# Queue order of the scan's loads, and GpSimd's part of a group norm a tick later

## Chip, cores and metric

The kernel runs on one core of a Trainium2 chip. The metric is the device time of one execution in microseconds (us), the median of several runs. Engines are named as the profile names them: PE (TensorE matmuls) and PEld (its weight loads), DVE (VectorE), ACT (ScalarE), POOL (GpSimd) and SP (SyncE, which issues nearly all DMAs).

## What is computed

Four layers on x of 4 images x 128 channels x 64 x 64 pixels, float32, each `x = x + layer(group_norm(x))`:

```
x = x + attention(gn(x))      # one head over 4096 pixels, 128 channels
x = x + conv5x5(gn(x))        # 25 taps, built from tables of weights
x = x + ssm(gn(x))            # 1x1 conv, two state-space scans, 1x1 conv
x = x + conv3x3(gn(x))
```

The third layer is what the change is about. Channels 0 to 63 run forward over the 4096 pixels, channels 64 to 127 backward; each channel has 64 states:

```
xc    = silu(causal_conv4(u))
delta = softplus(xc @ Wd + bd);  Bm = xc @ WB;  Cm = xc @ WC
h[t]  = exp(delta[t] * A) * h[t-1] + (delta[t] * xc[t]) * Bm[t]
y[t]  = sum over states (h[t] * Cm[t]) + D * xc[t]
```

## The kernel before

One program order is written out by hand (a manual schedule), and every engine runs its own queue in that order. There are two streams in it. `scan_core` (L1394) writes the scan, tick by tick. A generator, `images` in `program`, writes everything else ("the work"): attention, 5x5 convolution, the operands of the scan (`scan_prep`, `scan_operands`), and for images whose scan is over the last layer (`stage`, `end`, `back`).

**Ticks.** A tick is one step on a tile of 128 x 1024: 32 channels x 4 states on the partitions, 1024 pixels along. An image has 256 ticks: 4 chunks of pixels (c) x 2 directions (d) x 16 groups of states (q) x 2 groups of channels (g), g innermost. A "chunk-direction" (c, d) is thus 32 ticks. For tick i:

- `load` (L1428), on SP: for q = 0 the tiles `de` (delta) and `dx` (delta times xc) of this (c, d, g), each 512 KB, three buffers each; for g = 0 the rows `b` and `c` of B and C, 512 KB each, three buffers each, which serve two ticks; for q = 0 and g = 0 also `xc`, two DMAs of 128 KB into one tile.
- `drive` (L1469), on POOL: `db = dx * b` (L1472), three buffers.
- `decay` (L1454), on ACT: `da = exp(de * a)` (L1465) into PSUM.
- `recur` (L1474), on DVE: the scan `h = da * h + db` (L1482), and for two ticks of three the product with the C row (L1485).
- `weigh` (L1500), on POOL: that product for the other ticks (L1503); while PE has "wide" banks it is every i with i % 3 = 2.
- `collect` (L1505), on PE: sums over states (L1521), four ticks at a time; `keep` (L1490), on ACT, saves the last state of a chunk.

The loop at the end of `scan_core` (L1567) sets the order in step i, in short:

```
do(drive, i + 2); do(keep, i - 1); do(decay, i + 1, 0); do(recur, i)
do(weigh, i - 1); do(take, i - 4); do(preset, i - 4); do(collect, i - 3)
yield i
do(decay, i + 1, 1); do(load, i + AHEAD)      # AHEAD = 4
yield i
```

Within `load(i)` the order is de, dx (if q = 0), b, c (if g = 0), xc (if q = g = 0). Since each tile has a fixed number of buffers, a DMA into one waits until the last reader of what was in it is done; SP waits, and all DMAs written later wait behind it.

**The work between the ticks.** At each of the two yields of a step the driver adds half of `pace` to a credit and takes work until the credit is used; each piece of work yields its own cost in us. `PACES` gives the pace during the ticks of images 0 to 3. During the ticks of image b (b < 3), attention, convolution and operands of image b + 1 are written; during those of image 3, the last layers of images 0 to 2. When (b, "operands", c) is in `ready`, the operands of chunk c have been written; `before(b)` (L1782) is called four ticks before an image's first tick and takes work without ticks until the first chunk's operands are there.

**The group norm.** `group_norm` (L353) ends a long chain of small DVE instructions with a transpose `back` (L385), then two small products on POOL, `rs` (L387, a power of -0.5) and `nb` (L388), and yields. It is called for attention ("a"), the 5x5 convolution ("e"), the scan ("s") and the last layer ("m"). Nine of these calls fall among the ticks: e and s of images 1 to 3, m of images 0 to 2.

Of the kernel before, what the change touches and what calls it, by code (L numbers as in the profile page):

```python
# [32 lines left out]
P = 128  # L33
GROUPS = 32
GN_EPS = 1e-5
CH = 1024
MM = 512
HALF = P // 2
# [4 lines left out]

PRODUCT, VALUES, HOP, SLOT, AHEAD = 0.86, 0.9, 1.7, 0.7, 4
PACES = 2.65, 2.61, 2.6, 1.5


BQ, BK, BX, BP, CONVB, BD, DSKIP, MAINB, CONVW, ALOG = 0, 1, 2, 3, 4, 5, 6, 7, 8, 12  # L50
# [3 lines left out]
def conv_preact_kernel(  # L54
# [16 lines left out]
    nc = tc.nc  # L71
# [3 lines left out]
    NST = vecs.shape[1] - ALOG  # L75
    KC = 4
    SG, NI = 32, P // 32
# [14 lines left out]
    pools, ready = {}, set()  # L92
# [49 lines left out]
    NK, NQ = P // SG, NST // NI  # L142
# [167 lines left out]
    NRING = 8  # L310


    gn_work = const.tile([P, 2, 2 * 32], F32, name="gn_work")
    gn_sums = const.tile([P, 2, 32 // gsz], F32, name="gn_sums")

# [37 lines left out]
    def group_norm(st, name):  # L353


        def tile(tag, *shape):
            return small.tile([P, *shape], F32, tag=f"gn_{tag}", name=f"{tag}_{name}")

        by_sums = isinstance(st, Sums)
        if by_sums:  # L360
            st.aggregate()
        else:
            nc.vector.bn_aggr(gcols[:, :, 0], st.rearrange("p a b -> p (a b)"))
        turned, after = gn_work[:, 0], gn_work[:, 1]
# [12 lines left out]
        nc.vector.tensor_tensor(means, means, mean, ALU.add)  # L377
        nc.vector.tensor_tensor(means, means, means, ALU.mult)
        nc.vector.tensor_tensor(means, means, vars_, ALU.subtract if by_sums else ALU.add)
        total = gn_sums[:, 1]  # L380
        nc.vector.tensor_reduce(total, means, AX.X, ALU.add)
        wide = total.unsqueeze(2).to_broadcast([P, 32 // gsz, gsz])
        nc.vector.tensor_scalar(var, wide, 1.0 / gsz, GN_EPS, ALU.mult, ALU.add)
        back = tile("back", 2, 32)
        nc.vector.transpose(back.rearrange("p a b -> p (a b)"), after)  # L385
        rs, nb = tile("rs", 1), tile("nb", 1)
        nc.gpsimd.tensor_tensor(rs, back[:, 0, 0:1], mhalf, ALU.pow)  # L387
        nc.gpsimd.tensor_tensor(nb, back[:, 1, 0:1], rs, ALU.mult)  # L388
        yield HOP
        return rs, nb  # L390
# [30 lines left out]
    def attention_start(b, xn):  # L421

        if b == 0:
            st = stats_tile(f"a{b}")
            for i in range(NM):
                nc.vector.bn_stats(st[:, i, :], xn[:, bass.ts(i, MM)])
                yield 0.0
            gn = yield from group_norm(st, f"a{b}")
# [962 lines left out]
    KG = NK // 2  # L1391
    TICKS = NCH * 2 * NQ * KG

    def scan_core(mats4, ynds, before, widen, result):  # L1394


        ticks = [
            (b, c, d, q, g) for b in range(B)
            for c in range(NCH) for d in range(2) for q in range(NQ) for g in range(KG)
        ]  # L1400
        rows, rep, dbs, hcs, hold, yacc, xcs, last = {}, {}, {}, {}, {}, {}, {}, {}
# [21 lines left out]
        def at(i):  # L1423
            b, c, d, q, g = ticks[i]
            n = (d * KG + g) * NQ + q
            return slice(n, n + 1)

        def load(i):  # L1428
            b, c, d, q, g = ticks[i]
            (bmat, cmat), dd, dxd, xcd, _ = mats4[b]  # L1430
            if q == 0:
                assert (b, "operands", c) in ready
                for name, src in (("de", dd), ("dx", dxd)):
                    t = in_turn("rep", name, 3, [P, CH], f"{name}_{b}_{c}_{d}_{g}")
                    k = d * KG + g
                    src = src[c, k * SG : (k + 1) * SG].unsqueeze(1)
                    nc.sync.dma_start(t, src.to_broadcast([SG, NI, CH]))
                    rep[name, b, c, d, g] = t
            if g == 0:
                for name, src in (("b", bmat), ("c", cmat)):  # L1440
                    t = in_turn("rows", name, 3, [P, CH], f"{name}r_{b}_{c}_{d}_{q}")
                    n = d * NST + q * NI
                    nc.sync.dma_start(t, src[c, n : n + NI].unsqueeze(0).to_broadcast([SG, NI, CH]))
                    rows[name, b, c, d, q] = t
            if q == 0 and g == 0:
                t = in_turn("rows", "xc", 2, [P, MM], f"xcr_{b}_{c}_{d}")
                for h in range(CH // MM):
                    nc.sync.dma_start(
                        t[h * HALF : (h + 1) * HALF, :],
                        xcd[c, d * HALF : (d + 1) * HALF, bass.ts(h, MM)],  # L1450
                    )
                xcs[b, c, d] = t

        def decay(i, h):  # L1454
            b, c, d, q, g = ticks[i]
            if h == 0:
                das[i] = []
            elif "wide" in pools:
                return

            wide = "wide" in pools
            size = CH if wide else MM
            da = in_turn(*(("wide", "da", 2) if wide else ("s2", "half", 3)), [P, size], f"da_{i}_{h}")
            das[i].append(da)
            nc.scalar.activation(  # L1465
                da, rep["de", b, c, d, g][:, bass.ts(h, size)], AF.Exp, scale=a_neg[:, at(i)]
            )
# [93 lines left out]
        n = len(ticks)  # L1561

        def do(step, i, *args):
            if 0 <= i < n:
                step(i, *args)

        for i in range(-AHEAD, n + 4):  # L1567
            if (i + AHEAD) % TICKS == 0 and i + AHEAD < n:
                before((i + AHEAD) // TICKS)
            do(drive, i + 2)  # L1570
            do(keep, i - 1)
            late = i + 1 < n and i >= 0 and widen()
            if not late:
                do(decay, i + 1, 0)
            do(recur, i)
            if late:
                do(keep, i)
                late()
                do(decay, i + 1, 0)
            do(weigh, i - 1)  # L1580
            if i < n + 3:
                do(take, i - 4)
            do(preset, i - 4)
            do(collect, i - 3)
            yield i
            do(decay, i + 1, 1)
            do(load, i + AHEAD)
            yield i

    def scan_end(b, xs, st, yt, pieces):  # L1590
# [14 lines left out]
    def program(safe):  # L1605
        nonlocal more
        mats4, ynds, ends = {}, {}, {}
        ready.clear()
        ready.add("narrow")
        shared.clear()  # L1610
        if safe:
            nc.sync.dma_start(cs[:, :10, :], kept_sums)

        def load(tile, src):
            for c in range(NCH):
                nc.sync.dma_start(tile[:, bass.ts(c, CH)], src[:, bass.ts(c, CH)])
                yield 0.0
# [111 lines left out]
        with ExitStack() as es, tc.manual_schedule():  # L1729
# [49 lines left out]
            pools["hc"] = es.enter_context(tc.tile_pool(name=f"hc{safe}", bufs=8))  # L1779
            pace = PACES[0]  # L1780

            def before(b):  # L1782

                nonlocal pace
                while (b, "operands", 0) not in ready:
                    next(work)
                pace = PACES[min(b, len(PACES) - 1)]

            def result():

                while (B - 1, "staged") not in ready:
                    next(work, None)
                return ends[B - 1][2]

            credit = 0.0
            for i in scan_core(mats4, ynds, before, widen, result):
                if i % TICKS == 6 and i > TICKS:
                    ready.add((i // TICKS - 1, "scan"))
                if i == B * TICKS - TICKS // NCH + 6:
                    ready.update({(B - 1, "inner"), (B - 1, "lower")})  # L1800
                if i == B * TICKS - TICKS // NCH // 2 + 6:
                    ready.add((B - 1, "last"))
                credit = min(credit + pace / 2, pace)
# [22 lines left out]
    with tc.If(again > 0):  # L1826
        program(True)
# [59 lines left out]
```

## Time and profile before

| what | us |
|---|---|
| median of 3 runs (lowest, highest) | 4236.12 (4235.12, 4243.51) |
| the profiled execution | 4238.44 |
| its span in the profile | 4236.6 |
| first drive (L1472) starts | 675.0 |
| last drive starts | 4163.2 |
| POOL busy, of which drives and `weigh` | 3523.4, of which 2394.9 and 832.6 |
| DVE busy, of which scans of the four common forms and products | 3557.1, of which 2311.5 and 828.8 |
| PE busy | 3683.7 |

DMAs: 512 each of the b and c rows, 64 each of de and dx, all of 512 KB; one queue (q1 on the page) moves 736.99 MB of 740.97. The median time from issue to landing is 5.5 us for b, 4.2 for c, 5.2 for de, 6.4 for dx.

How to read the profile: it is one execution. A line of the waits reads "engine, output, line <- what ended the wait: us in total, times, longest". A line of the windows has the stretch, its length, then busy time and number of instructions of PE, PEld, DVE, ACT, POOL, the granted clock of PE, the share of the DMA engines and GB/s. A line of the timeline has the start, the time from start to end, engine, line, operation and tiles, how many equal instructions were merged, and in brackets the idle time before it and what ended it. Ends of matmuls are modelled, and spans on POOL are rough.

### The profile page before, as it was taken

What the parts mean: (1) busy time and instruction counts of PE and PEld (TensorE: products, weight loads), DVE (VectorE), ACT (ScalarE), POOL (GpSimd) and SP (SyncE); (2) the same over time, 40 slices, a digit from 0 to 9 for tenths busy, and PEclk for the clock granted to TensorE, in tenths of its full rate; (3) what the DMA queues carried; (4) which work ended last, traced back from release to release, by engine and by line L of the source; (5) the groups of instructions that cost most, each with busy time, mean ns of one, the idle gap of its engine ahead of it and who ended that gap; (6) DMA issues with size and microseconds to landing.
All of it is one profiled execution on the core that took longest, in us unless ns stands there. A gap on an engine that the chain in (4) does not pass through costs nothing. (4 is left out here: it accounts for less than half of the span.)

```text
span 4236.6 us, 49519 instructions
## 1 busy us (share of the span) xinstructions
PE 3683.7 (87%) x17628; PEld 2133.7 (50%) x17628; DVE 3557.1 (84%) x2554; ACT 2332.4 (55%) x3910; POOL 3523.4 (83%) x1683
## 2 busy tenths in 40 slices
PE   8999998999999879999999889999898466575666
PEld 4444444888883338887753267787633122121212
DVE  3832216999999979999999899999998899999996
ACT  3344316666664476666653766666645554544442
POOL 2533316999999979999999899999998899999995
PEclk9999999999999989999999999999999688787877
DMA  1120006555555576555555655555555755666562
GB/s 66 47 91 21 3 20 246 195 184 194 193 192 192 180 259 202 192 194 186 196 183 180 241 207 183 196 187 192 191 184 204 250 199 200 218 203 234 188 227 74
DMA packets 223725, 740.97 MB, mean 175 GB/s; under 512 B 29662, under 2 KB 30942, under 8 KB 223212
## 3 DMA queue, kind: packets, MB, share of 16 engines
q1 hardware_dynamic: 221548, 736.99, 50.1%
q8 instruction: 140, 2.29, 0.2%
q14 instruction: 117, 0.96, 0.1%
q10 hardware_dynamic: 1920, 0.73, 0.1%
HBM read 662.14 MB, written 75.47 MB: 174 GB/s over the span
## 5 line engine op out<-in xcount | busy, mean ns | idle before, releaser
L1472 POOL TENSOR_TENSOR db<-dx,br 128x1024 f32<-128x1024 f32 x1024 | 2394.9, 2367 | 170.3 <-DMA dx<-dxd 71.7
L1465 ACT ACTIVATE da<-de,a_neg 128x1024 f32<-128x1024 f32 (+1 forms) x1091 | 1161.5, 1065 | 396.5 <-DVE hc L1485 272.3
L1482 DVE TENSOR_TENSOR_SCAN da<-da,last,db 128x1024 f32<-128x1024 f32 (+1 forms) x501 | 1149.4, 2294 | 48.4 <-POOL db L1472 38.4
L1485 DVE TENSOR_TENSOR hc<-da,cr 128x1024 f32<-128x1024 f32 (+1 forms) x708 | 828.8, 1171 | 63.4 <-DVE da L1482 1.4
L1521 PE MATMUL y<-hc,sel 128*32 128x512 f32 x4096 | 609.0, 649 | 305.9 <-POOL hc L1503 226.1
L1503 POOL TENSOR_TENSOR hc<-hc,cr 128x1024 f32<-128x1024 f32 x352 | 832.6, 2365 | 4.4 <-ACT last L1498 3.0
L696 PE MATMUL sc<-r,x 128*128 128x256 f32 x3072 | 806.4, 388 | 27.6 <-ACT exchange L709 16.4
L717 PEld LDWEIGHTS acc<-v,exchange 128*128 128x128 f32 x6144 | 802.1, 192 | 46.4 <-issue 10.0
L717 PE MATMUL acc<-v,exchange 128*128 128x129 f32 x6144 | 804.8, 275 | 0.0
L696 PEld LDWEIGHTS sc<-r,x 128*128 128x128 f32 x3072 | 532.0, 192 | 191.9 <-ACT last L1498 41.1
L1482 DVE TENSOR_TENSOR_SCAN hc<-da,last,db 128x1024 f32<-128x1024 f32 (+1 forms) x267 | 596.0, 2232 | 6.1 <-POOL db L1472 5.5
L709 ACT ACTIVATE exchange<-sc 128x512 f32<-128x512 f32 x768 | 444.2, 589 | 225.5 <-PE sc L696 216.5
L1521 PEld LDWEIGHTS y<-hc,sel 128*32 128x32 f32 x4096 | 115.2, 113 | 658.2 <-POOL hc L1503 322.1
L1482 DVE TENSOR_TENSOR_SCAN da<-da,db 128x1024 f32<-128x1024 f32 (+1 forms) x171 | 376.6, 2203 | 22.7 <-ACT da L1465 12.9
L518 POOL TENSOR_TENSOR sidep<-sidep,exchange 128x512 f32<-128x512 f32 x120 | 172.6, 1439 | 245.2 <-ACT exchange L500 242.8
L1498 ACT COPY last<-da 128x1 f32<-128x1 f32 x512 | 80.5, 157 | 518.0 <-DVE hc L1485 517.2
L500 ACT ACTIVATE exchange<-sc 128x512 f32<-128x512 f32 x256 | 152.6, 596 | 253.7 <-PE sc L499 248.9
L518 DVE TENSOR_TENSOR sided<-sided,exchange 128x512 f32<-128x512 f32 x120 | 98.7, 823 | 211.6 <-ACT exchange L500 210.5
L506 PE MATMUL acc<-exchange,v 128*128 128x512 f32 x512 | 261.9, 594 | 0.9
L499 PE MATMUL sc<-r,x 128*128 128x512 f32 x512 | 262.0, 594 | 0.6 <-ACT r L482 0.6
L861 PE MATMUL pcm<-xpm,cs 128*128 128x512 f32 x432 | 211.0, 637 | 41.3 <-ACT xpm L393 41.3
L1482 DVE TENSOR_TENSOR_SCAN hc<-da,db 128x1024 f32<-128x1024 f32 (+1 forms) x85 | 189.5, 2230 | 5.7 <-ACT da L1465 5.7
(266 smaller groups left out, 3062.0 us busy)
## 6 DMA issues: line engine op xcount, KB each, us to landing
br<-bm SPq DMA_DIRECT2D x512, 512.0 KB, 5.5
cr<-cm SPq DMA_DIRECT2D x512, 512.0 KB, 4.2
de<-dd SPq DMA_DIRECT2D x64, 512.0 KB, 5.2
dx<-dxd SPq DMA_DIRECT2D x64, 512.0 KB, 6.4
xs<-in_x_dram SPq DMA_DIRECT2D x16, 512.0 KB, 7.4
xsd<-xs SPq DMA_DIRECT2D x16, 512.0 KB, 6.1
xcd<-xc SPq DMA_DIRECT2D x16, 512.0 KB, 4.6
bm<-bs SPq DMA_DIRECT2D x32, 256.0 KB, 5.3
```

The costliest lines, as they stand in the source:

```text
L499: nc.tensor.matmul(sc, xn[:, bass.ts(j, P)], rq[blk], start=True, stop=True)
L506: nc.tensor.matmul(acc[blk], v[:, j, :C], ring[:, u % NRING, :], start=j == 0, stop=j == NJT - 1)
L518: eng.tensor_tensor(s, s, ring[:, u % NRING, :], ALU.add)
L696: nc.tensor.matmul(sc[:, bass.ts(n, HM)], xn[:, bass.ts(2 * k + n, P)], rq[blk][:, cut], start=True, stop=True,)
L709: nc.scalar.activation(pt, sc, AF.Exp)
L717: nc.tensor.matmul(acc[part][:, bass.ts(t, CV)], ring[:, u % NRING, n * HM + t * P : n * HM + (t + 1) * P], v[:, 2 * k + n, :], start=(k, ...
L1465: nc.scalar.activation(da, rep["de", b, c, d, g][:, bass.ts(h, size)], AF.Exp, scale=a_neg[:, at(i)])
L1472: nc.gpsimd.tensor_tensor(dbs[i], rep["dx", b, c, d, g], rows["b", b, c, d, q], ALU.mult)
L1482: nc.vector.tensor_tensor_scan(h, da, db[:, cut], before, ALU.mult, ALU.add)
L1485: nc.vector.tensor_tensor(hc[:, cut], h, rows["c", b, c, d, q][:, cut], ALU.mult)
L1503: nc.gpsimd.tensor_tensor(hcs[i], hcs[i], rows["c", b, c, d, q], ALU.mult)
L1521: nc.tensor.matmul(y[r : r + SG, :], sel, hcs[first + gg][:, bass.ts(h, MM)], start=False, stop=q == NQ - 1, tile_position=(0, r), skip_gr ...
```

## The change

There are three parts, and new paces.

1. `load` is split into `steps` (de and dx), `row` (one row of B or C) and itself. B rows are written two ticks earlier (`load(i)` writes the B row of tick i + 2). The dx of the second tick of a chunk-direction is written one load earlier, ahead of xc and of its de. The dx and de of a chunk-direction's first tick are written up to eight ticks earlier than before (EARLY), if the chunk's operands have been written.
2. `group_norm` yields ahead of its two POOL products until the loop has begun another tick (`ticks_begun`), if ticks are running.
3. `PACES` changes from 2.65, 2.61, 2.6, 1.5 to 2.65, 2.62, 2.62, 1.55.

```diff
-PRODUCT, VALUES, HOP, SLOT, AHEAD = 0.86, 0.9, 1.7, 0.7, 4
-PACES = 2.65, 2.61, 2.6, 1.5
+PRODUCT, VALUES, HOP, SLOT, AHEAD, EARLY = 0.86, 0.9, 1.7, 0.7, 4, 8
+PACES = 2.65, 2.62, 2.62, 1.55
...
         rs, nb = tile("rs", 1), tile("nb", 1)
+        begun = ticks_begun[0]
+        while begun and ticks_begun[0] == begun:
+            yield 0.4
         nc.gpsimd.tensor_tensor(rs, back[:, 0, 0:1], mhalf, ALU.pow)
...
+        PART = NQ * KG
+        def made(i):
+            b, c, d, q, g = ticks[i]
+            return (b, "operands", c) in ready
+        def steps(i, *names):
+            b, c, d, q, g = ticks[i]
+            for name in names:
+                if (name, b, c, d, g) in rep:
+                    continue
...
+                nc.sync.dma_start(t, src.to_broadcast([SG, NI, CH]))
+                rep[name, b, c, d, g] = t
+        def row(i, name):
+            b, c, d, q, g = ticks[i]
+            if g > 0 or (name, b, c, d, q) in rows:
+                return
...
         def load(i):
+            for j in (i, i + 2):
+                if j < n and made(j):
+                    row(j, "b")
+            if i >= n:
+                return
             b, c, d, q, g = ticks[i]
             if q == 0:
-                for name, src in (("de", dd), ("dx", dxd)):
...
-            if g == 0:
-                for name, src in (("b", bmat), ("c", cmat)):
...
+                steps(i, "dx", "de")
+            row(i, "c")
             if q == 0 and g == 0:
+                steps(i + 1, "dx")
                 t = in_turn("rows", "xc", 2, [P, MM], f"xcr_{b}_{c}_{d}")
...
+            first = i // PART * PART + PART
+            if first - i <= EARLY and first < n and made(first):
+                steps(first, "dx", "de")
...
             do(drive, i + 2)
+            ticks_begun[0] = i + AHEAD + 1 if i < n + 3 else 0
...
-            do(load, i + AHEAD)
+            if i + AHEAD >= 0:
+                load(i + AHEAD)
```

`before` and `result` set `ticks_begun[0]` to 0, so that no norm waits for a tick while the loop stands.

More of the change, by code (lines that the diff above doesn't have):

```diff
@@ L310, in conv_preact_kernel @@
     NRING = 8
+    ticks_begun = [0]
     gn_work = const.tile([P, 2, 2 * 32], F32, name="gn_work")
@@ L1426, in at @@
             return slice(n, n + 1)
-        def load(i):
+        PART = NQ * KG
[7 more added lines that the diff above has]
+                    continue
+                src = mats4[b]["de dx".split().index(name) + 1]
+                t = in_turn("rep", name, 3, [P, CH], f"{name}_{b}_{c}_{d}_{g}")
+                k = d * KG + g
+                src = src[c, k * SG : (k + 1) * SG].unsqueeze(1)
+                nc.sync.dma_start(t, src.to_broadcast([SG, NI, CH]))
+                rep[name, b, c, d, g] = t
@@ new lines, in row @@
+        def row(i, name):
+            b, c, d, q, g = ticks[i]
+            if g > 0 or (name, b, c, d, q) in rows:
+                return
+            t = in_turn("rows", name, 3, [P, CH], f"{name}r_{b}_{c}_{d}_{q}")
+            n = d * NST + q * NI
+            src = mats4[b][0]["bc".index(name)][c, n : n + NI].unsqueeze(0)
+            nc.sync.dma_start(t, src.to_broadcast([SG, NI, CH]))
+            rows[name, b, c, d, q] = t
+        def load(i):
+            for j in (i, i + 2):
[3 more added lines that the diff above has]
+                return
+            assert made(i)
@@ L1429, in load @@
             b, c, d, q, g = ticks[i]
-            (bmat, cmat), dd, dxd, xcd, _ = mats4[b]
             if q == 0:
-                assert (b, "operands", c) in ready
-                for name, src in (("de", dd), ("dx", dxd)):
[L1434 to L1438, printed above, removed]
@@ L1439, in load @@
-            if g == 0:
-                for name, src in (("b", bmat), ("c", cmat)):
[L1441 to L1444, printed above, removed]
+                steps(i, "dx", "de")
+            row(i, "c")
             if q == 0 and g == 0:
+                steps(i + 1, "dx")
                 t = in_turn("rows", "xc", 2, [P, MM], f"xcr_{b}_{c}_{d}")
@@ L1449, in load @@
                         t[h * HALF : (h + 1) * HALF, :],
-                        xcd[c, d * HALF : (d + 1) * HALF, bass.ts(h, MM)],
+                        mats4[b][3][c, d * HALF : (d + 1) * HALF, bass.ts(h, MM)],
                     )
                 xcs[b, c, d] = t
+            first = i // PART * PART + PART
+            if first - i <= EARLY and first < n and made(first):
+                steps(first, "dx", "de")
         def decay(i, h):
@@ L1609, in program @@
         ready.add("narrow")
+        ticks_begun[0] = 0
         shared.clear()
@@ L1784, in before @@
                 nonlocal pace
+                ticks_begun[0] = 0
                 while (b, "operands", 0) not in ready:
@@ L1789, in result @@
             def result():
+                ticks_begun[0] = 0
                 while (B - 1, "staged") not in ready:
```

## Prediction

> **What bounds the kernel now.** I began with busy time by engine, then split the span by stage, then read who waits for whom, then one stall in order of time. The page:
>
> ```profile
> PE 3683.7 (87%) x17628; PEld 2133.7 (50%) x17628; DVE 3557.1 (84%) x2554; ACT 2332.4 (55%) x3910; POOL 3523.4 (83%) x1683
> ```
>
> The shares are averages over a head without scan (0 to 675 us), the scan of 1024 ticks (first drive at 675.0, last at 4163.2, so 3.41 us a tick) and a tail of 72 us. The change touches the scan alone. Busy time there by stretch (attention of images 1, 2 and 3, then the last image's ticks):
>
> ```profile
> 730.00:1290.00 560.00, 554.74 (x3829) 450.92 (x3831) 539.33 (x309) 385.63 (x699) 545.26 (x236) 1.00 0.56 194
> 1610.00:2160.00 550.00, 541.50 (x3716) 438.15 (x3715) 528.65 (x304) 376.62 (x684) 535.50 (x231) 1.00 0.56 193
> 2480.00:3045.00 565.00, 551.33 (x3756) 444.65 (x3754) 538.75 (x309) 380.07 (x688) 545.11 (x236) 0.99 0.55 190
> 3340.00:4165.00 825.00, 510.76 (x1610) 153.22 (x1613) 789.87 (x466) 391.09 (x621) 781.30 (x355) 0.79 0.61 211
> ```
>
> The columns after the length are PE, PEld, DVE, ACT, POOL. PE, DVE and POOL all stand at 95 to 99% in attention; at the end PE is at 62% and DVE and POOL share the load. So a wait taken from one engine is worth only what the other two leave. The waits of POOL and DVE:
>
> ```profile
> POOL db L1472 <- DMA dx<-dxd: 71.7, 27, 4.9
> POOL db L1472 <- DMA br<-bm: 46.1, 20, 5.2
> POOL rs_e L387 <- DVE back_e L385: 20.4, 4, 9.6
> DVE da L1482 <- POOL db L1472: 45.5, 36, 2.8
> DVE pb L1306 <- ACT u L1335: 51.6, 24, 6.0
> DVE da L1482 <- ACT da L1465: 24.3, 20, 2.5
> ```
>
> In the scan POOL idles 215 us by the timeline's gaps, DVE 152 us in waits and 68 us in gaps under 150 ns. POOL waits for DVE 28 us, DVE for POOL only 45.5 + 5.5 (its `hc` form) + 1.6 = 52.6 us. Reading: POOL starves, makes it good with its lead of up to two ticks, and DVE notices about a third. DVE's chain without waits for POOL is some 52 us shorter, and **that, not POOL's 145 us of stalls on dx, br and norms, is the ceiling of the gain** as long as DVE's other waits stay.
>
> One stall in time, SP first, then POOL, around tick 352 (a chunk-direction, of 32 ticks, begins there):
>
> ```profile
> 1871.12 0.51 SPq L1443 DMA_DIRECT2D cr<-cm  x1
> 1871.68 1.24 SPq L1448 DMA_DIRECT2D xcr<-xcd  x2
> 1873.02 0.55 SPq L1437 DMA_DIRECT2D de<-dd  x1
> 1873.61 0.60 SPq L1437 DMA_DIRECT2D dx<-dxd  x1
> ```
> ```profile
> 1868.74 2.35 POOL L1503 TENSOR_TENSOR hc<-hc,cr 128x1024 f32<-128x1024 f32 x1
> 1871.05 4.70 POOL L1472 TENSOR_TENSOR db<-dx,br 128x1024 f32<-128x1024 f32 x2
> 1879.68 2.35 POOL L1472 TENSOR_TENSOR db<-dx,br 128x1024 f32<-128x1024 f32 x1 [3.93 <-DMA dx<-dxd]
> ```
>
> SP stands at the C row of tick 352 until the `weigh` of tick 347 frees its buffer at 1871.1. Behind it come xc (two), de and dx of tick 353; dx lands 6.07 us after its issue, 8.5 us after the release. POOL meanwhile has two drives, 4.7 us. The stall is the difference. It comes back at ticks 65, 97, 129, 161 and so on, always the second tick of a chunk-direction, in a period of three: about 4.3 us where the pooled tick leaves two operations in between, 2.9 and 1.0 us where it leaves three.
>
> [...] SP waits 1520 us for `weigh` (319 times) at L1443 and then issues three to six DMAs in a burst. [...] Here 2.32 us against the mean of 2.367, and I use 2.32. [...] The scan reads `da` from PSUM, and lasts 2.33 us beside the stalled POOL and 2.35 us beside the busy one: a POOL that idles less doesn't slow DVE.
>
> **The change part by part.**
>
> *dx of a chunk-direction's second tick* goes one load earlier, straight behind the C row: xc (1.24 and 0.1 us) and de (0.6 us) no longer stand in front, 1.9 us. Its buffer is freed by the drive two ticks before the chunk, which POOL runs before the `weigh` that frees the C row: no later release, or about 1 us where DVE frees it. It shares the DMA engines with the C row alone, as a B row behind its C row does, 5.5 us by the median of landings against 6.4 for dx. So it lands 0.56 + 5.5 = 6.1 us after the release: 6.1 - 4.64 = 1.4 us of stall in the worst third, 0 to 0.5 in the others. POOL: 71.7 to some 20 us.
>
> *First steps eight ticks ahead.* They use the third buffer, free since the chunk-direction before: no wait. They cost one megabyte at another time, some 3 us of transfers in a queue where DMA stands at 55%; the B rows behind have five ticks (16 us) in hand. At image borders they are read soon after their write, and SP may stand for one landing (3.0 us); C rows have four ticks.
>
> *B rows two ticks ahead* wait for the drive of the last tick that used the buffer, one tick earlier than the `weigh` SP stops at anyway. POOL's 46 us on br falls to perhaps 20. Most lies at image borders (1501 to 1600, 2378 to 2470), where DVE waits for ACT, so I count little of it.
>
> *What DVE gets.* In the DVE timeline, its waits for POOL that follow a dx stall sum to 34.7 us; those that follow the e and s norms to 11.3; the rest 6.6. Stalls of 76 us gave 34.7, so the lead swallows about 1.3 us of each; of stalls of 1.4 us hardly any is left: **-32 us**, keeping 2.7.
>
> *POOL's part of the norm.* Today `rs` stands before the next drive and POOL waits 2.7 to 4.6 us (nine times in the scan by the timeline, 10.8 + 9.0 + 8.0 = 27.8 us; the waits above have head and tail in them) until DVE has been through the norm's chain. After: one drive (2.32) and sometimes a `weigh` (2.32) lie in between: 0 to 2 us left. Of 11.3 us DVE keeps about 2: **-9 us**. The price: the work beside the scan yields until the next tick, half a tick on average, at most one (3.3 us) for each norm, while PE idles. All nine norms are followed by convolutions or operands, with 9 to 38% of PE free (171.94 of 190 us busy from 1290, 510.76 of 825 at the end); and the paces 2.62, 2.62, 1.55 give back 0.4%, 0.8% and 3.3%, 1, 2 and 8 ticks of 256.
>
> *Rest.* Start of the scan and single br stalls: **-3**; image borders **-2** (bounds 0 and -10).
>
> *What is late next.* ACT's decays behind PE. PE has 5.3, 8.5 and 13.7 us free in the attention stretches; DVE gains there 3.3, 3.3 and 6.6; the paces take 2 us (0.38% of 550) and 4 us (0.77% of 565) from the second and third. No trace shows what ACT loses when PE has under 1% left; bounds 0 and 19 us (all 13 of the gain and the 6 of the paces). I take **+8**.
>
> Sum: -32 - 9 - 3 - 2 + 8 = **-38 us** on 4238.4 us of the profiled execution (span 4236.6 and 1.8 around it): 4200. The median of the runs lies 2.3 us below it: **4198 us**, -0.9%.
>
> **The rivals.**
>
> *Half the effect.* dx still leaves with the C row; if it lands 6.4 us after its issue and its release lags by 1 us on DVE's side, only 1 us of each stall goes, DVE gets 15 instead of 32, and the paces cost what PE can't give. 4236 - 15 - 9 - 3 + 8 = 4217. For it: even the shortest dx landing took 5.2 us, over the two drives. Against: the de in front of it is gone.
>
> *All of it.* No PE friction, and the borders give 10 more: With the leftovers of dx and norms (5) gone as well: 4198 - 8 - 8 - 5 = 4177.
>
> *Slower: the slack before the image borders is used up.* The loop must have an image's first operands four ticks before its first tick (L1785), or it drains the other work while POOL and DVE stand. POOL's timeline puts the first L1319 of image 1 behind drive 251, written at i = 249 and due at 252; images 2 and 3 behind 506 and 762, due at 508 and 764, written at 504 and 760. Two norms can slip the work by two ticks and image 0's pace stays at 2.65. From three ticks of slip on, each tick costs its 3.2 us and a restart (the first ticks of the scan stood 4.3 + 0.8 us for DMAs and some 5 us for ACT): two ticks over make 16 us a border, 49 for three, against the 38 gained: 4236 + 49 - 38 = 4247. Against: the mean slip is one tick, and images 1 and 2 get one and two ticks back by the pace.
>
> **How the numbers follow.** Forecast 0.62, half 0.16, all 0.05, slower 0.17. The half case reaches to within 0.2% (8.5 us, about what a measurement of this kernel can tell from no change) with 0.07. So faster 0.76, same 0.07, slower 0.17. The range 4178 to 4246 leaves out most of the slower case and part of "all". With the unknown of +8 at both ends (0 and 19) the forecast alone is 4190 to 4209.
>
> **What would show it.** After: POOL's wait for dx under 30 us, its waits for `rs` in the scan under 10, DVE's for POOL near 10 and not moved to ACT's `da` (36 us of both forms now); SP with C row, dx, xc, xc, de in that order; POOL waiting for DVE more (28 us now), as its lead fills. Wrong if DVE waits for ACT 20 us more in the attention stretches, or if a gap of several ticks stands on both engines at 256, 512 or 768.

## The result, and the profile after

| what | before | after |
|---|---|---|
| median (lowest, highest) of 4 runs each, side by side | 4239.42 (4235.12, 4243.51) | 4211.88 (4208.06, 4214.73) |
| ratio, 95% interval | | 0.9935 (0.9917 to 0.9952) |
| profiled execution, its span | 4238.44, 4236.6 | 4214.73, 4212.9 |
| first to last drive (the scan) | 3490.5 wide | 3465.1 wide |

The kernel is 27.5 us faster; 38 were forecast. By the spans the gain is 23.7 us, all of it in the scan (25.4). In the page of the kernel after, the line of busy times holds the first surprise: DVE, whose waits were to shrink, is 24.8 us busier (3581.9 less 3557.1). It has the same scans to do, and four products more: POOL has 348 of its `weigh` instead of 352, and DVE's products take 834.1 us instead of 828.8. That explains 5.3 us of the 24.8.

```profile
PE 3684.3 (87%) x17628; PEld 2132.3 (51%) x17628; DVE 3581.9 (85%) x2561; ACT 2334.0 (55%) x3911; POOL 3519.0 (84%) x1679
```

These are the stretches of the kernel after, in the columns that the prediction explained. The third and fourth end a little earlier than before, since the scan does; read them as shares of their length. PE stays at 99% in attention and DVE is at 98% (before 96%) in the last stretch.

```profile
730.00:1290.00 560.00, 555.84 (x3839) 453.34 (x3837) 540.94 (x311) 386.74 (x698) 548.53 (x237) 1.00 0.59 196
1610.00:2160.00 550.00, 545.69 (x3753) 443.55 (x3755) 534.50 (x307) 382.07 (x690) 540.24 (x234) 1.00 0.58 195
2480.00:3020.00 540.00, 535.97 (x3684) 433.83 (x3683) 520.29 (x299) 372.43 (x673) 526.58 (x228) 1.00 0.57 189
3340.00:4140.00 800.00, 521.01 (x1613) 154.07 (x1610) 781.66 (x457) 384.38 (x612) 772.82 (x350) 0.78 0.63 212
```

These are the waits of the kernel after. A line of them covers the whole execution, with the wait before the very first drive in it, which ends with a different load from kernel to kernel. Here it is 11.9 of the 31.4 us for dx; in the scan alone POOL waits 19.5 us for dx.

```profile
POOL db L1502 <- DVE hc L1512: 38.9, 47, 3.1
POOL db L1502 <- DMA dx<-dxd: 31.4, 11, 11.9
POOL db L1502 <- DVE da L1512: 30.7, 20, 5.3
POOL rs_m L391 <- DVE back_m L386: 20.3, 4, 12.5
POOL rs_e L391 <- DVE back_e L386: 18.2, 4, 9.6
POOL rs_s L391 <- DVE back_s L386: 11.8, 4, 4.4
DVE da L1512 <- POOL db L1502: 10.2, 11, 2.5
DVE da L1512 <- ACT da L1495: 35.6, 27, 3.2
DVE pb L1310 <- ACT u L1339: 44.3, 21, 6.0
```

There are three readings. POOL's wait for dx in the scan is down from 71.7 us to 19.5, and its wait for br has left the list. DVE's wait for POOL is down from 52.6 us to 10.4 (10.2 for scans that write `da`, 0.2 for those that write `hc`). But POOL still waits for the norm's `back`: 23.7 us for the nine norms among the ticks, against 27.7 before, though a whole tick was put between.

The stall at tick 352 once more (ticks 352 and 353 are a chunk-direction's first two), now in the SP timeline and the POOL timeline of the kernel after:

```profile
1870.39 0.51 SPq L1457 DMA_DIRECT2D cr<-cm  x1
1870.96 0.60 SPq L1447 DMA_DIRECT2D dx<-dxd  x1
1871.60 1.24 SPq L1475 DMA_DIRECT2D xcr<-xcd  x2
1872.94 0.55 SPq L1447 DMA_DIRECT2D de<-dd  x1
```
```profile
1868.01 2.36 POOL L1533 TENSOR_TENSOR hc<-hc,cr 128x1024 f32<-128x1024 f32 x1
1870.33 4.69 POOL L1502 TENSOR_TENSOR db<-dx,br 128x1024 f32<-128x1024 f32 x2
1875.97 2.37 POOL L1502 TENSOR_TENSOR db<-dx,br 128x1024 f32<-128x1024 f32 x1 [0.95 <-DMA dx<-dxd]
```

SP is released at 1870.39, by the end of the `weigh` at 1870.37, as before. Behind the C row it now issues dx at once: 0.57 us after the release instead of 2.49. The drive of tick 353 waits 0.95 us instead of 3.93.

So the loads did in the main what they were to do, and the norm did not. Where does the rest of DVE's added busy time come from? The chain of 13 small DVE instructions in a norm (L344 to L385 before, L345 to L386 after), taken from its first start to its last end and summed over the nine norms among the ticks, took 31.5 us before and takes 51.2 now. This is one norm in the DVE timeline of the kernel after (an m, between the scans of ticks 944 and 945), and beside it the POOL timeline of the same stretch:

```profile
3889.06 0.17 DVE L345 TENSOR_REDUCE gn_sums<-su_m 128x2 f32<-128x16 f32 x1 [0.66 <-ACT junk L338]
3889.27 5.00 DVE L346 TENSOR_SCALAR gcols<-gn_sums 128x2 f32<-128x2 f32 x1
3894.30 0.16 DVE L347 TENSOR_TENSOR aw_m<-gcols,aw_m 128x1 f32<-128x1 f32 x1
...
3896.58 0.25 DVE L386 STREAM_TRANSPOSE back_m<-gn_work 128x64 f32<-128x64 f32 x1
```
```profile
3889.61 2.34 POOL L1502 TENSOR_TENSOR db<-dx,br 128x1024 f32<-128x1024 f32 x1
3891.90 2.34 POOL L1533 TENSOR_TENSOR hc<-hc,cr 128x1024 f32<-128x1024 f32 x1
3896.91 0.55 POOL L391 TENSOR_TENSOR rs_m<-back_m,mhalf 128x1 f32<-128x1 f32 x1 [2.66 <-DVE back_m L386]
```

Two columns of numbers are scaled, with 2 elements a row: an instruction that takes 0.17 us elsewhere stands in the profile as 5.00 us *busy*. It ends at 3894.27. POOL's `weigh` ends at 3894.24, and POOL then stands, because `rs` needs the end of this very chain. Then the other eleven instructions run in 0.16 to 0.25 us each. The reading to test is that L346 couldn't proceed while POOL was at its drive and its `weigh`; below I call such an instruction held. If so, the wait of the change lets POOL run two long instructions ahead of `rs`, these hold the chain up, and POOL then waits 2.66 us for the rest of it anyway.

### The profile page after: what moved, and what is told of

Same layout as the page of the kernel before. It is cut to its first block, busy times and chain, and to the rows that moved or that the text cites. A ratio compares the mean times of both kernels' runs of the same rounds, so it can differ in the third digit from the quotient of the medians.

```text
span 4212.9 us, 49863 instructions
## 1 busy us (share of the span) xinstructions
PE 3684.3 (87%) x17628; PEld 2132.3 (51%) x17628; DVE 3581.9 (85%) x2561; ACT 2334.0 (55%) x3911; POOL 3519.0 (84%) x1679
## 3 DMA queue, kind: packets, MB, share of 16 engines
q1 hardware_dynamic: 221548, 736.99, 51.8%
## 5 line engine op out<-in xcount | busy, mean ns | idle before, releaser
L1515 DVE TENSOR_TENSOR hc<-da,cr 128x1024 f32<-128x1024 f32 (+1 forms) x714 | 834.1, 1168 | 62.7 <-issue 0.9
L1533 POOL TENSOR_TENSOR hc<-hc,cr 128x1024 f32<-128x1024 f32 x348 | 823.2, 2366 | 14.4 <-ACT last L1528 11.9
L1512 DVE TENSOR_TENSOR_SCAN da<-da,db 128x1024 f32<-128x1024 f32 (+1 forms) x175 | 381.4, 2179 | 24.4 <-ACT da L1495 17.2
```

Source lines behind the costliest of these rows:

```text
L1512: nc.vector.tensor_tensor_scan(h, da, db[:, cut], before, ALU.mult, ALU.add)
L1515: nc.vector.tensor_tensor(hc[:, cut], h, rows["c", b, c, d, q][:, cut], ALU.mult)
L1533: nc.gpsimd.tensor_tensor(hcs[i], hcs[i], rows["c", b, c, d, q], ALU.mult)
```

## The experiments

My theory: the wait in the norm costs time, 8 to 15 us by the first expectation, since GpSimd's drives beside the chain hold up DVE's small instructions in SBUF; the loads alone are then worth more than the whole change. Rivals: the wait costs by the delay of the work (a norm's results reach PE and ACT a tick later), or the change merely uses up POOL's lead over DVE, without a single cause, or the loads gained less than forecast and the norm did no harm. Times are medians; a difference is to the kernel before, run beside it on the same chip (4238.81, 4240.58 or 4237.58).

| kernel | us | ratio (95%) | to before |
|---|---|---|---|
| after, without the norm's wait | 4188.71 | 0.9877 (0.9862 to 0.9892) | -50.1 |
| before, with the norm's wait | 4243.95 | 1.0012 (1.0005 to 1.0018) | +5.1 |
| after, norm's chain in PSUM | 4192.59 | 0.9885 (0.9870 to 0.9900) | -46.2 |
| the same without the wait | 4187.78 | 0.9877 (0.9861 to 0.9892) | -51.0 |
| before, with dx ahead | 4204.09 | 0.9911 (0.9897 to 0.9924) | -36.5 |
| before, with B rows ahead | 4259.31 | 1.0040 (1.0026 to 1.0053) | +18.7 |
| before, with first steps ahead | 4225.82 | 0.9963 (0.9950 to 0.9977) | -14.8 |
| before, with the new paces | 4238.59 | 0.9995 (0.9987 to 1.0004) | -2.0 |
| without norm's wait and B rows | 4194.81 | 0.9901 (0.9884 to 0.9917) | -42.8 |
| without norm's wait, 128 tensor_scalar | 4320.69 | 1.0194 (1.0177 to 1.0211) | +83.1 |
| without norm's wait, 128 tensor_reduce | 4194.85 | 0.9899 (0.9883 to 0.9916) | -42.7 |
| after, norm's wait doubled | 4225.11 | 0.9969 (0.9957 to 0.9982) | -12.5 |

### The norm's wait, taken away and put alone

The kernel after without its wait:

```diff
-        begun = ticks_begun[0]
-        while begun and ticks_begun[0] == begun:
-            yield 0.4
         nc.gpsimd.tensor_tensor(rs, back[:, 0, 0:1], mhalf, ALU.pow)
```

> The changed kernel with the group norm's wait for the next tick taken out; loads and paces as changed. Theory (held by POOL): in the changed kernel's nine norms in the scan DVE's chain grew from 31.5 to 51.2 us because two of its small operations (L346, L347) sit out running POOL operations, while POOL's wait for rs stayed at 23.7 us. Then the chains go back to some 32 us and the time falls 8 to 15 us below the changed kernel's, to about 4200. Rival (the norm part worked as forecast, and the gain was lost elsewhere): the time rises 9 us, to about 4221.

Measured: 4188.71 us, a gain of 50.1 over before where the whole change gives 27.5. The nine chains take 31.9 us (31.5 before, 51.2 after), DVE is 31.2 us less busy in the scan than after (3264.41 and 3295.65; the chains are 19.3 of it), and POOL waits 31.4 us at `rs` again. The norm's wait costs 23 us in this kernel, more than the theory had asked for; the prediction had it bring 9.

The kernel before with the same three lines, and `ticks_begun` set as in the change:

> The kernel before with the group norm's wait for the next tick alone; loads and paces as before. Held by POOL: chains of DVE of some 50 us in sum over the nine norms, POOL's wait for rs in the scan still over 20 us, and 5 to 15 us slower than before, about 4250. Rival (the norm part worked as forecast): 9 us faster than before, about 4230.

Measured: 4243.95 us, 5.1 slower, a loss that is small and at the lower end of what was expected. The chains take 53.5 us, 22 us more than before, where the change has 20 us more. Why 22 us of hold cost 5 here and 20 cost 23 there is argued, not shown: the kernel before has slack to lose, since DVE's waits for POOL fall from 52.6 to 41.8 us while it is busier, so half of the hold may only take the place of an idle time. In the change the loads have used up that slack. POOL's wait for `rs` falls by 3.8 us (27.7 to 23.9), not to nothing.

### Is it the place of the operands? The chain in PSUM

If GpSimd holds the chain up through SBUF, which no trace so far shows, then tiles in a PSUM bank must free it with the wait left in place; if the delay of the work is what costs, nothing changes. The chain's tiles go into a bank; a memset and a copy on DVE are added for each norm.

```diff
+            one = bank("z", f"gn_{name}")
+            gcols_ = one[:, 0:64].rearrange("p (a b) -> p a b", a=2)
+            nc.vector.memset(one[:, 0:64], 0.0)
+            st.aggregate(gcols_, one[:, 64:66])
...
+            turned = one[:, 128:192]
+            nc.vector.transpose(turned, one[:, 0:64])
...
+            nc.vector.tensor_copy(away, means)
+            nc.vector.tensor_tensor(square, means, away, ALU.mult)
+            nc.vector.tensor_tensor(means, square, vars_, ALU.subtract)
```

> The changed kernel, wait for the next tick kept, with the small tiles of the norms by sums in a PSUM bank, so that no operation of the chain reads two tiles of SBUF or copies SBUF to SBUF in fp32 by tensor_scalar (one copy and one memset of DVE more for each norm). Held by POOL: no long operation is left in the chain (under 4 us each, 32 in sum), POOL comes to rs when DVE is done (under 10 us of wait in the scan), and the time falls some 20 us below the changed kernel's, to about 4190. Rival (the long operations have another cause, such as a semaphore or a late reader): chains stay near 50 us and the time within 5 us of the changed kernel's, or 1 to 3 us above for the two operations more.

Measured: 4192.59 us; 19.3 of the 23 us are back, with the wait still there. Neither the delay of the work nor a used-up lead would give that. The same norm (m) in the DVE timeline of this kernel, and the POOL timeline beside it:

```profile
3873.51 0.17 DVE L346 TENSOR_SCALAR gn_m<-gn_m 128x2 f32<-128x2 f32 x1
3873.72 0.16 DVE L347 TENSOR_TENSOR aw_m<-gn_m,aw_m 128x1 f32<-128x1 f32 x1
...
3876.30 0.25 DVE L400 STREAM_TRANSPOSE back_m<-gn_work 128x64 f32<-128x64 f32 x1
```
```profile
3874.27 2.38 POOL L1516 TENSOR_TENSOR db<-dx,br 128x1024 f32<-128x1024 f32 x1
3876.57 2.38 POOL L1547 TENSOR_TENSOR hc<-hc,cr 128x1024 f32<-128x1024 f32 x1
3878.87 0.59 POOL L405 TENSOR_TENSOR rs_m<-back_m,mhalf 128x1 f32<-128x1 f32 x1
```

L346 and L347 take 0.17 and 0.16 us beside the drive before, which ends at 3873.99. POOL's next drive runs from 3874.27 and nine of the chain's instructions run beside it at 0.19 to 0.25 us each. `back` is done at 3876.55, under the drive, and `rs` follows the `weigh` with no wait at all. All nine chains together take 29.2 us, 3.24 each, and POOL's waits for `rs` sum to 5.8 us instead of 23.7. This is what the step "POOL's part of the norm" of the prediction had in mind; it needs the wait and the chain out of GpSimd's way.

The same kernel without the wait:

> As e7, without the wait for the next tick. Held by POOL: chains near 32 us, POOL waits for rs some 27 us as before the change, time 3 to 5 us under e1's (the few operations held there as well), about 4197, and above e7's. Rival: as e1, within 2 us.

Measured: 4187.78 us, not told apart from 4188.71 with the chain in SBUF, as the rival had it. Without the wait POOL stands at `rs` (30.9 us) and so holds little: the chains take 31.9 us in SBUF and 29.2 in PSUM. The wait's other effects together, the tick of delay against the freed POOL, cost 4.8 us (4192.59 less 4187.78). So even the wait that works brings no gain.

### The suspected cost by itself

128 instructions of the held form, on two columns of a tile that nobody else uses, one for every eighth tick, in the kernel without the norm's wait:

```diff
+            if i % 8 == 4:
+                nc.vector.tensor_scalar(probe[:, 0], probe[:, 1], 0.5, None, ALU.mult)
```

> As e1, with one tensor_scalar more of DVE on 128x2 float32 from SBUF to SBUF behind the products of every eighth tick (128 in all); its result is read by nothing. Held by POOL: its duration is not the 0.17 us that it takes in the head but 1 to 2 us by the mean, up to 5, as POOL is busy 94% of the scan; the time rises by 100 to 250 us over e1's. Rival (only something special to the norm's place makes it long): 0.2 us each, 25 us in all.

And the same number of tensor_reduce, which reads the same 128 x 2 elements:

```diff
-                nc.vector.tensor_scalar(probe[:, 0], probe[:, 1], 0.5, None, ALU.mult)
+                nc.vector.tensor_reduce(probe[:, 0, 0:1], probe[:, 1], AX.X, ALU.add)
```

> As e10, with a tensor_reduce of the same 128x2 tile instead, one input of SBUF, which was never long in the norm's chain (L345 of the changed kernel: 0.16 to 0.17 us). Held by POOL through the operation's kind: 0.17 us each, 20 to 30 us over e1. Rival (any small operation of DVE waits there): as long as the tensor_scalar of e10.

Measured: 132 us more for the tensor_scalar (4320.69 to 4188.71), 6.1 more for the tensor_reduce, less than the 20 to 30 expected. The line of each probe by source, first in the kernel with tensor_scalar, then with tensor_reduce (least, median and most ns, the stretch, the forms):

```profile
L1519 DVE TENSOR_SCALAR probe<-probe x128: 141/1269/10078, 709.6 to 4241.5; 128x2 f32<-128x2 f32 x128
```
```profile
L1519 DVE TENSOR_REDUCE probe<-probe x128: 127/144/147, 713.1 to 4116.1; 128x1 f32<-128x2 f32 x128
```

Neither needs long for its 128 x 2 numbers: the shortest tensor_scalar took 0.141 us, and the reductions 0.127 to 0.147. The tensor_scalar takes 1.27 us by the median, 1.35 in the mean, and once 10.08, longer than four of POOL's drives (2.37 us in the mean of the kernel after). In the timelines, 95 of the 128 take over 0.2 us, and each of these ends within 0.03 us of the end of a POOL instruction; of the 128 reductions 108 lie under POOL's instructions, and none of them is longer for it. The tensor_scalars sum to 173 us, against 132 us of added time. So with the same 128 x 2 input the operation made the difference here, 10.08 against 0.147 us at most; the size alone did not.

### The loads, one by one

dx of the second tick behind the C row, alone, in the kernel before:

```diff
+                    if (name, b, c, d, g) in rep:
+                        continue
...
+                t = in_turn("rep", "dx", 3, [P, CH], f"dx_{b}_{c}_{d}_1")
+                src = dxd[c, (d * KG + 1) * SG : (d * KG + 2) * SG].unsqueeze(1)
+                nc.sync.dma_start(t, src.to_broadcast([SG, NI, CH]))
+                rep["dx", b, c, d, 1] = t
```

> The kernel before, with one part: the dx of a chunk-direction's second tick is written one load earlier, behind that load's C row and ahead of xc and of its de. If this part carries the gain of the loads, as the prediction has it (32 of 37 us): POOL's wait for dx falls from 72 to 20 to 30 us, DVE's for POOL from 53 to 25 or less, and the time by some 30 us, to about 4209. Rival (the gain of 50 us that the loads showed comes from first steps and B rows as much): 15 us or less.

Measured: -36.5 us. POOL's wait for dx falls to 15.5 us in the scan. A part comes back as a wait for the B row that is now the later one: 12.4 us before the third drive of a chunk-direction, where there was none. In all the wait for br in the scan grows only from 46.1 to 52.2 us, since 12.3 of the 64.4 us in these waits lie before the first drive:

```profile
POOL db L1478 <- DMA br<-bm: 64.4, 32, 12.3
DVE da L1488 <- POOL db L1478: 30.2, 22, 2.8
```

B rows two ticks ahead, alone: `load(i)` writes the B row of i + 2 first.

```diff
+            for j in (i, i + 2):
+                if j < len(ticks):
+                    brow(j)
...
-                for name, src in (("b", bmat), ("c", cmat)):
+                for name, src in (("c", cmat),):
```

> The kernel before, with one part: each B row is written two ticks earlier. Prediction: POOL's wait for br falls from 46 us to 20 or less, but DVE, which waits for ACT there, gains 2 to 5 us: about 4235. Rival (B rows carry part of the surplus): 10 us or more faster.

Measured: +18.7 us. The waits of this kernel, POOL and DVE, then SP:

```profile
POOL db L1485 <- DMA dx<-dxd: 86.8, 28, 13.6
DVE da L1495 <- POOL db L1485: 57.4, 45, 2.8
```
```profile
SPq L1435 <- POOL db L1485: 1306.1, 427, 11.6
```

SP now stops at the B row, 427 times, for the drive that frees its buffer, and de and dx of a chunk-direction's first tick stand behind it. In the SP timeline at tick 352, and the POOL timeline:

```profile
1878.69 0.51 SPq L1435 DMA_DIRECT2D br<-bm  x1
1879.25 0.60 SPq L1450 DMA_DIRECT2D de<-dd  x1
1879.90 1.05 SPq L1450 DMA_DIRECT2D dx<-dxd  x1
1883.32 0.51 SPq L1456 DMA_DIRECT2D cr<-cm  x1
```
```profile
1893.58 2.36 POOL L1485 TENSOR_TENSOR db<-dx,br 128x1024 f32<-128x1024 f32 x1 [5.43 <-DMA dx<-dxd]
```

Before, these two were issued 9 us ahead of the C row (1862.3 and 1871.1); here 4 us (1879.25 and 1883.32). They now stand close ahead of the loads behind them, and the stall of tick 353 grows from 3.93 to 5.43 us. It isn't the only one: away from the image borders (the eight ticks on either side of ticks 256, 512 and 768 left out), POOL's idle time before the first two drives of a chunk-direction sums to 100.9 us, against 74.6 before. (The line for dx alone would not show it: 13.6 of its 86.8 us lie before the first drive.)

The first steps eight ticks ahead, alone:

```diff
+            first = i // 32 * 32 + 32
+            if first - i <= 8 and first < len(ticks):
+                b, c, d, q, g = ticks[first]
+                if (b, "operands", c) in ready and ("dx", b, c, d, g) not in rep:
...
+                        nc.sync.dma_start(t, src.to_broadcast([SG, NI, CH]))
+                        rep[name, b, c, d, g] = t
```

> The kernel before, with one part: dx and de of a chunk-direction's first tick are written up to eight ticks earlier. Prediction: costs nothing and alone brings nothing, 4236 within 5. Rival (two transfers less in the burst at the border let the second tick's dx land sooner): POOL's wait for dx falls by a third or more, and the time by 10 us or more.

Measured: -14.8 us. One megabyte less is queued at each border between chunk-directions. POOL's waits for dx and br fall from 71.7 and 46.1 us to these, in the waits of this kernel:

```profile
POOL db L1483 <- DMA dx<-dxd: 49.1, 23, 5.2
POOL db L1483 <- DMA br<-bm: 30.1, 14, 4.4
```

The paces alone:

```diff
-PACES = 2.65, 2.61, 2.6, 1.5
+PACES = 2.65, 2.62, 2.62, 1.55
```

> The kernel before, with the new paces alone. Prediction: up to 6 us slower (0.4% and 0.8% more work of PE for each tick in two attention stretches). Rival (a pace moves where the operands fall between the ticks, and that is worth something by itself): 5 us or more faster.

Measured: -2.0 us with an interval on both sides of nothing.

The three parts and the paces sum to -34.6 us when each is alone, and to -50.1 together. The last kernel of this group, which shows where the 15 us lie, takes the B rows' lead out of the one without the norm's wait:

```diff
-            for j in (i, i + 2):
+            for j in (i,):
```

> As e1 (changed loads and paces, no wait in the norm), but each B row written where it was before, not two ticks earlier. If B rows are worth something once the first steps are out of their way: POOL's wait for br comes back (46 to 64 us in the runs that keep it) and the time rises 5 us or more above e1's 4188.7. If they are of no use, as br stalls fall where DVE waits for ACT: within 3 us of e1. If they cost here as they did alone (19 us): faster than e1 by 5 us or more.

Measured: 4194.81 us, 6.1 more than with the B rows ahead, at the edge of what these runs tell apart. POOL's waits for br are back in the waits of this kernel:

```profile
POOL db L1499 <- DMA br<-bm: 38.6, 24, 5.4
POOL db L1499 <- DMA dx<-dxd: 27.2, 12, 10.1
```

So the same edit costs 18.7 us alone and brings about 6 where the first steps are written early: in that order of the queue they no longer stand behind a B row. The other three gain less together than alone: dx, first steps and paces sum to -53.3 us one by one and bring 42.8 here.

### The norm's wait doubled

```diff
-        begun = ticks_begun[0]
-        while begun and ticks_begun[0] == begun:
-            yield 0.4
+        for _ in range(2):
+            begun = ticks_begun[0]
+            while begun and ticks_begun[0] == begun:
+                yield 0.4
```

> The changed kernel with the norm's wait doubled, two ticks instead of one. Held by POOL: POOL has a drive and perhaps a product more to run before it comes to rs and lets DVE through; the nine chains grow from 51 us to 70 or more in sum, and the time by 15 us or more over the changed kernel's 4212. Rival (the wait costs by PE's idle tick): chains stay at 51 us, and the time rises 4 us, the difference between e7 and e8.

Measured: 4225.11 us, 13.2 above the kernel after by the medians. The nine chains grow from 51.2 to 56.7 us, not to the 70 that my theory asked for, and POOL's wait for `rs` is gone (0.0). But POOL's idle time is not gone. It has moved to the drive, as in the POOL timeline of this kernel at one of the m norms, whose chain ends at 3439.90:

```profile
3434.96 2.37 POOL L1534 TENSOR_TENSOR hc<-hc,cr 128x1024 f32<-128x1024 f32 x1
3442.17 2.35 POOL L1503 TENSOR_TENSOR db<-dx,br 128x1024 f32<-128x1024 f32 x1 [4.85 <-DVE da L1513]
```

The drive needs a buffer that the next scan frees, and that scan stands behind the chain in DVE's queue. So POOL soon runs out of work that doesn't need DVE, and the chain gets through then. By the timelines POOL stands still for 24.4 us of the nine chains before, 22.6 after, 24.6 without the wait, 22.7 with two ticks of it, and 5.0 with one tick and the chain in PSUM. That is why more delay hardly lengthens the chains, and why neither length of the wait fills POOL's idle time while the chain is in SBUF.

Most of the 13 us must then come from the second tick of delay; that is by elimination, not shown. DVE's waits for ACT's `u` and `pt` in the operands are 61 us here against 37.6 after, but they are 51.6 without any wait, so they don't simply grow with the delay. The rival, that delay costs, may have a part here which it doesn't have at one tick (4.8 us at most).

## Why the prediction was right and wrong

**The direction was right, and the ceiling nearly.** DVE's waits for POOL were named as the ceiling, 52 us. With the loads alone the time falls by 50.1, close to it. But DVE's waits for POOL fall only from 52.6 to 15.3 us; all its waits in the scan fall from 151.9 to 105.8, and its busy time by 6.2. Some 15 us thus came from places that the ceiling left as they were.

**dx of the second tick: right in the main.** -32 forecast, -36.5 measured alone; the order of SP and POOL's dx wait under 30 us (19.5) came as written. The stall was to be 1.4 us at most: it is 0.95 at tick 353, but four of the ten that stay take 2.4 to 5.3 us (ticks 257, 449, 513 and 641). The rival "half the effect" would have put the total at 4217, close to the 4211.88 measured, but by a mechanism that the trace excludes: not half but nearly three quarters of the dx stalls are gone. A right-looking number belonged to the wrong reason.

**First steps and B rows: mis-sized, with opposite signs.** "They cost one megabyte at another time" gave no gain (its 3 us of transfers are an estimate, from 736.99 MB in 50.1% of the span of 4236.6 us); what was left out is that the same megabyte no longer stands in front of the rows at the border: -14.8 alone, with POOL's waits for dx and br down by 22.6 and 16.0 us. The B rows' wait was said to come one tick earlier than one "SP stops at anyway". That holds for B and C rows, but not for the de and dx that stand behind a B row once it is written first: +18.7 alone, and about -6 only because the first steps had left. Loads and paces together brought 50, where the terms (-32, -3, -2) gave 37.

**The norm: this step failed.** "After: one drive (2.32) and sometimes a `weigh` (2.32) lie in between: 0 to 2 us left" took the chain's length for a constant (2.32 us is the time from the start of a drive to that of what follows it without a gap, by the median of the kernel before). It wasn't while POOL worked: 31.5 us became 51.2 and the `rs` waits went from 27.7 to 23.7 us instead of under 10. Forecast -9, cost +23. The prediction had looked at DVE beside a busy POOL for the scan alone, found 2.33 us beside a stalled one and 2.35 beside a busy one, and took from it that a POOL that idles less doesn't slow DVE. That wasn't shown for anything but the scan. The eleven small instructions between the reduction and `back`, with all operands in SBUF, were counted as free. The kernel before had shown it: there L345 (the same tensor_scalar) took up to 2142 ns. These are its instances by source, before and after (least, median, most ns):

```profile
L345 DVE TENSOR_SCALAR gcols<-gn_sums x12: 169/170/2142, 493.2 to 4178.5; 128x2 f32<-128x2 f32 x12
```
```profile
L346 DVE TENSOR_SCALAR gcols<-gn_sums x12: 169/597/5002, 493.8 to 4154.1; 128x2 f32<-128x2 f32 x12
```

The median of 170 ns hides it; the greatest shows it. In 4 of the 9 norms before the change this instruction took 0.77 to 2.14 us: a drive or a `weigh` was under way, and each time it ended within 0.03 us of the end of POOL's last instruction ahead of `rs`, where POOL then stood. POOL's idle time at `rs`, which the change set out to fill, was what DVE's chain ran in. For POOL the wait then freed 4 us (27.7 to 23.7 at `rs`) and not 18 or more.

By kind of instruction, the runs show this. The tensor_scalar took up to 5.00 us in the norm (L346 of the kernel after) and 10.08 in the probe. The tensor_tensor L347, with two SBUF inputs, took up to 2.26 us, against 0.16 where it wasn't held. The tensor_reduce took at most 0.147 us in the probe, and 0.16 to 0.17 at L345 in the nine norms after, in eight of them beside a drive or a `weigh`. In those norms 13 instructions of the chains took over 0.3 us, all of them L346 or L347, and each ended within 0.04 us of the end of a POOL instruction. What follows L347 in the chain (0.18 to 0.25 us) met no drive and no `weigh` in the kernels before and after, so these two traces don't show whether it would be held. With the tiles in PSUM the nine chains took 3.24 us each.

**PE friction: not seen.** +8 was taken for decays that come late behind a fuller PE. DVE's waits for ACT's `da` are 38.0 us in both forms, 36.4 before, and 13.6 in the three attention stretches together, 17.0 before, with PE busy for 555.84 of 560 us in the first. With the 13 us that the loads brought beyond their terms it makes 8 + 13 = 21 us better than forecast, and the norm 23 + 9 = 32 us worse: the total is 11 us short of -38. That it came so near is luck: two errors, each nearly as large as the gain or larger, cancelled for the most part.

**The slower rival did not come.** No gap of several ticks stands on both engines at image borders: within twelve ticks of 256, 512 and 768 DVE's longest idle time is 3.3, 3.2 and 3.4 us, about one tick (5.8, 5.7 and 4.8 before), and POOL's longest before a drive is 5.3 (5.2 before).

**What stays open.** Why one chain is held for one drive and the next for two isn't settled: every probe of over 0.2 us ends with a POOL instruction, but not always with the first, since the 5.00 us from 3889.27 cover the whole drive from 3889.61 and the whole `weigh` behind it. No run tells when a hold ends with the first and when later. And the 4.8 us that the tick of delay costs once the chain is free, net of what POOL gains, weren't traced to a wait. A rival that no run tests: the delayed work also shifts which engine takes a product. With the chain in PSUM, POOL has 348 of them with the wait and 351 without it, so that DVE has 4.3 us more of products in the scan (831.5 and 827.2), about as much as the loss.

The version that beats both kernels is the change without the norm's wait: 4188.71 us, 50 us below before and 23 below after (4187.78 with the chain in PSUM as well, no different).

## What to carry to other kernels

Here one engine's idle time was what another lived on, and filling it cost 23 us (4211.88 less 4188.71). So before filling a wait of GpSimd, list the DVE instructions that will then run beside it and look at their greatest duration in the trace (2.14 us before the change), not only their median (0.17). When loads are moved in a queue, ask of each place what stands behind it when it stops for its buffer; the same move cost 18.7 us in one order and brought about 6 in another. And check a total by its terms: the result here came near to one rival's number while its terms were off by 21 us in one direction and 32 in the other.

## What was not expected of the hardware

A DVE instruction on 128 x 2 numbers in SBUF stood as busy for 5.00 us in the norm, beside a GpSimd that was busy without a break, and for 10.08 us in the probe, against 0.17 and 0.14 us when free. The loss is entered as busy time of that instruction and not as a wait, so that the waits alone say that DVE got better: 151.9 to 101.7 us in the scan, with 25.0 us more busy time beside it, 19.7 of them in the nine chains. And 512 KB loads in a queue whose packets take 52% of the span of the 16 DMA engines land 3.9 to 6.0 us after their issue (medians of the four kinds after; 4.2 to 6.4 before).
